# A two-layer graph attention kernel: the first part written as a hand-ordered pipeline of node tiles, with list work in pieces between them

## The chip, the cores and the metric

The kernel runs on one core of a Trainium2 chip. A core has a matrix engine (TensorE, PE in the profile; its weight loads are PEld), VectorE (DVE), ScalarE (ACT), GpSimd (POOL) and SyncE (SP), which here only issues DMAs. All engines run their own instructions in order and wait for each other through semaphores; DMAs move data between the device memory and the on-chip SBUF. The metric is the device time of one execution in microseconds (us). The time before is 2451.34 us, the median of 9 runs (2443.16 to 2461.27).

## The reference

There are 3125 nodes with 768 features each, and 53125 directed edges (each of 25000 pairs both ways, and a self loop per node), sorted by destination. What is computed, without the parameters' shapes:

```python
h  = relu(layernorm(x))                     # 3125 x 768
xl = h @ W1                                 # 3125 x 1024, 4 heads of 256
e  = leaky_relu((xl.a_src1)[src] + (xl.a_dst1)[dst], 0.2)
alpha = softmax of e over the edges with one dst
g  = segment_sum(xl[src] * alpha, dst) + b1
h1 = relu(layernorm(g) * g1 + be1) + (h @ Wr1 + br1)
# second layer: the same with W2 (1024 x 768) and one head
out = x + layernorm(gat(h1)) * g2 + be2 + (h1 @ Wr2 + br2)
```

## The kernel before, in words

The nodes are cut into 25 tiles of 125 (P = 125, NB = 25), and each tile gets a window of S = 2304 edge slots, 18 columns (J) of 128. The work of the first layer goes through these stages.

**First part (L586 to L669).** For each node tile, `transposed(b)` computes mean and variance on DVE (`norm_stats`: L316, L318), the square root on ScalarE (L322), the reciprocal and the scaling on DVE (L326, L600), transposes the tile on PE (L604) and takes the relu on ScalarE into `h0` (L606). Eight tiles `xt` are loaded ahead; the load of tile b + 8 is issued when tile b has been transposed. `alphas(b)` multiplies the transposed tile by the folded attention vectors `wa1` (L614, 12 matmul records) and copies 8 columns into `asad1` (L616). `products()` is a generator of 100 steps, four to a tile; one step is three chunks of `h @ W1` for one half of the tile's 1024 columns (L626, six matmul records). After each half ScalarE copies it into `row` (L629, two buffers), and a full row is stored to `table1` by SP (L146, L147); whole groups of `h0` go to `h0T_d` (L634).

Beside the tiles the first part holds three other pieces of work:
- `edge_list` (L197): loads `dst` and `src`, casts them, counts on DVE how many destinations lie below each tile (25 times L218, then L221 and L222), sums the counts with one matmul (L226), sets `starts` and the flag (L228 to L240), and splits the sources (L242 to L246).
- `fold` (L295): `wa1` from W1 and the attention vectors. For each of six chunks of W1 and each of two vectors GpSimd multiplies 128x1024 elements (L300), and ScalarE sums each of four heads (L304).
- `windows` (L248): SP reads each tile's start into a register (L177) and issues two list loads (L256, L257), 50 in all. DVE casts them (L260), PE transposes them (L263), DVE copies them back (L264) and computes the slots' indices (L266 to L271), and `keep` is stored four times (L277).

The order of PE's instructions is the written one (`manual_schedule(engines={PE})`, L641). The other engines' instructions are ordered by the framework's scheduler, which takes what is ready and prefers what was written earlier. Written order: the edge list's loads, four tiles with two product steps, the rest of the edge list, the fold, ten product steps, then tiles 4 to 24, each with the alphas of the tile four before and one product step; `windows` stands ahead of tile 12. So 33 product steps are written in the first part.

**Softmax (L332, called at L671).** A loop over 25 tiles loads two broadcast lists, compares them with node numbers on DVE (L374, L376, L379, L381), picks values with matmuls (L391, L399) and reduces on DVE (L393, L396, L401); then come scans over all slots (L452 to L479) with PE transposes between (L433, L444). Product steps are interleaved: one or two for a tile, then 8, 2, 8 and 2. What is left of them follows at L678.

**Between softmax and the sums.** W2 is folded on DVE in the pool "wf" (L681 to L691), which ends ahead of L693. Then comes the residual product of the first four tiles (L693 to L700): eight products of `wr1` and `h0[0]` into three PSUM buffers `pm` (L698). `copy_residual` copies each on ScalarE into the staging tile `rt` (L576), which belongs to the pool `mp` and has one buffer for two products, and every second copy is followed by four stores (L580). SP issues all of these loads and stores.

**Sums (L485, called at L782)**: GpSimd gathers the rows of `table1` for each column of slots (L524), ScalarE and DVE scale them (L542, L543), PE adds them up by one-hot matrices (L547, L559); the residual product of the other tiles runs between (L728). Its pools open after the first part's pools have closed. The second layer has the same stages.

A pool takes the place on top of those that are open, and a pool that opens after another has closed takes its place; unless it has `reuse_waits="tile"`, its first use waits for all work on the closed pool's tiles.

Of the kernel before, what the change touches and what calls it, by code (L numbers as in the profile page):

```python
# [58 lines left out]
def in_order(  # L59
# [137 lines left out]
    def edge_list(ep, pe):  # L197
# [18 lines left out]
        for b in range(NB):  # L216
            less = ep.tile([P, F], BF16, name="less", bufs=3)
            nc.vector.tensor_scalar(less, d16, float(b * P), 0.0, op0=OP.is_lt, op1=OP.add,  # L218
                                    accum_out=cnt[:, b:b + 1])
# [6 lines left out]
        nc.tensor.matmul(p_c[:1, :NB + 1], ones, cnt, start=True, stop=True)  # L226
        tot = ep.tile([1, NB + 1], F32, name="tot")
# [12 lines left out]
        nc.vector.tensor_copy(flag, flag_f)  # L240
        s_f = ep.tile([P, F], F32, name="s_f")
# [6 lines left out]
    def windows(pe):  # L248

        with tc.tile_pool(name="wn", bufs=1) as ep:  # L250
# [7 lines left out]
            for t, to in ((k16, dst_s), (s16, src_s)):  # L258
                tf = ep.tile([NB, S], F32, name="tf")
                nc.vector.tensor_copy(tf, t)  # L260
                pt = pe.tile([128, 512], F32, name="pe")
                for j in range(J):
                    nc.tensor.transpose(pt[:, j * NB:(j + 1) * NB], tf[:, j * 128:(j + 1) * 128], ident[:NB, :NB])  # L263
                nc.vector.tensor_copy(to.rearrange("p (b j) -> p j b", j=J),  # L264
# [4 lines left out]
            nc.vector.tensor_copy(idx_s, src_s)  # L269
            q, _ = divided(ep, src_s, [128, NB * J], "sh")  # L270
            nc.vector.tensor_copy(hi_s, q)  # L271

            keep = ep.tile([NB, S + 2], BF16, name="keep")
# [21 lines left out]
    def fold(abs_, w, nk, heads, cols, to):  # L295

        for k in range(nk):
            for m in range(2):
                t = abs_[2 + m % (len(abs_) - 2)]
                nc.gpsimd.tensor_tensor(t, w[:, k, :heads * cols], abs_[m], OP.mult)  # L300
                t = t.rearrange("p (h c) -> p h c", h=heads)
                for h in range(heads):
                    o = m * heads + h
                    nc.scalar.activation(t[:, h, :], t[:, h, :], AF.Copy, accum_out=to[:, k, o:o + 1])  # L304

    def norm_stats(pool, z, n):

        for _ in norm_steps(pool, z, n):
            pass
        return norm_steps.found  # L310
# [260 lines left out]
    with tc.tile_pool(name="m1", bufs=1) as mp:  # L571
# [10 lines left out]
        with tc.tile_pool(name="w1", bufs=1) as wp, tc.tile_pool(name="pm1", bufs=1, space=PSUM) as pm1:  # L582
# [3 lines left out]
            with tc.tile_pool(name="d1", bufs=2) as dp, tc.tile_pool(name="pd1", bufs=1, space=PSUM) as pp:  # L586
# [6 lines left out]
                def transposed(b):  # L593
# [5 lines left out]
                    mu, rstd = norm_stats(dp, xt, D)  # L599
                    nc.vector.tensor_scalar(xt, xt, mu, rstd, op0=OP.subtract, op1=OP.mult)  # L600
# [9 lines left out]
                def alphas(b):  # L610
# [5 lines left out]
                    nc.vector.tensor_copy(asad1[:, b, :], pa)  # L616
# [21 lines left out]
                AHEAD = 8  # L638
                EARLY = 4
                order = ctx.enter_context(ExitStack())  # L640
                order.enter_context(tc.manual_schedule(engines={PE}))  # L641
                with tc.tile_pool(name="el", bufs=1) as ep:
                    for b in range(2):
                        fetch(b)
                    listed = edge_list(ep, pp)
                    next(listed)
                    for k in range(NK1):
                        (nc.scalar, nc.gpsimd)[k % 2].dma_start(w1[:, k, :], W1[k * 128:(k + 1) * 128, :])
                    for b in range(2, AHEAD):
                        fetch(b)  # L650
                    abs1 = folded(mp, H, C1, a_src1, a_dst1, "wr1", 2)
                    for b in range(EARLY):
                        transposed(b)
                        if b == EARLY - 1:
                            for _ in range(2):
                                next(fill)
                    for _ in listed:
                        pass
                fold(abs1, w1, NK1, H, C1, wa1)
                for _ in range(10):  # L660
                    next(fill)
                for b in range(EARLY, NB):
                    if b == 12:
                        windows(pp)
                    transposed(b)
                    alphas(b - EARLY)
# [675 lines left out]
```

## Time and profile before

| what | us |
|---|---|
| median of 9 runs | 2451.34 |
| the profiled execution, its own time | 2454.62 |
| its span, first to last instruction | 2452.8 |
| mean granted PE clock, share of full | 0.955 |
| PE busy over the span | 2245.8 |
| DVE busy | 1921.4 |
| ACT busy | 1299.5 |
| POOL busy | 1174.4 |

The profile is of one execution. Its first table gives the busy time of each engine, and its second cuts the span into 40 slices of 61.3 us with the busy share of each engine in tenths (9 is 90% or more); PEclk is the clock that PE was granted. In lists of stretches each engine's busy time is followed by its number of instructions in brackets. In lists of waits the waiting instruction stands left of the arrow and what ended the wait right of it, with the sum, the number of times and the longest; "SPq" is SP's queue of DMA issues. An fp32 matmul shows as two records. The first part lies from 0 to 225 us, softmax from 225 to 490, the residual product of the first four tiles from 510 to 550.

### The profile page before, as it was taken

The numbers are of one execution on the slowest core, as the hardware profiler recorded it, in microseconds if no ns is written. First come the engines' busy times: TensorE is split into PE (matmuls) and PEld (weight loads), VectorE is DVE, ScalarE is ACT, GpSimd is POOL, SyncE is SP. The second block draws the span as 40 slices with busy tenths as digits, with TensorE's granted clock in tenths as the row PEclk, the third lists the DMA queues.
The fourth block names the chain that finished last, engine by engine and source line by source line (L and its number), as shares of the span: only waits on it lengthen the run. The fifth ranks groups of instructions, "written<-read, shape, count | busy, mean of one in ns | idle before, by whom it ended". The sixth has DMA issues, their size and how long they took to land.

```text
span 2452.8 us, 35967 instructions
## 1 busy us (share of the span) xinstructions
PE 2245.8 (92%) x11254; PEld 1481.3 (60%) x11254; DVE 1921.4 (78%) x4304; ACT 1299.5 (53%) x2783; POOL 1174.4 (48%) x995
## 2 busy tenths in 40 slices
PE   4858999998999999999999999799898999998987
PEld 2446655445666666666666776466565666666665
DVE  7433999847888888898989999587677687777777
ACT  3312332217888888888888898001244444444443
POOL 4200000015656555555655775000477777777775
PEclk9868999998999999999999999899999999998998
DMA  4235553269888888888988897784688988888886
GB/s 159 87 109 180 192 194 106 90 219 334 306 297 315 300 311 303 299 316 284 324 283 310 320 337 273 288 296 161 203 307 307 314 302 301 297 297 298 291 284 212
DMA packets 185506, 637.94 MB, mean 260 GB/s; under 512 B 31924, under 2 KB 49189, under 8 KB 184542
## 3 DMA queue, kind: packets, MB, share of 16 engines
q0 software_dynamic: 104464, 422.46, 49.9%
q1 hardware_dynamic: 76564, 201.94, 23.5%
q10 hardware_dynamic: 4282, 11.18, 1.3%
q8 instruction: 93, 1.52, 0.2%
q14 instruction: 103, 0.84, 0.1%
HBM read 567.40 MB, written 68.08 MB: 259 GB/s over the span
## 4 chain that ended last, share of the span: by engine, by line
PE 70%; DVE 16%; issue 5%; DMA 4%; ACT 2%; POOL 1%; SPq 1%; DVEq 0%; another core or an unknown queue 0%; ACTq 0%; POOLq 0%
PE pa L547 21%; PE p L773 11%; PE pa L559 8%; PE pr L728 8%; PE pr L807 7%; PE pm L626 6%; DVE g L543 3%; DVE scr L393 2%; DVE al L396 2%; PE pm L698 2%; PE pas L614 1%; DMA g<-table,idx_s 1%; PE pq L391 1%; PE pa L563 1%; DMA bs<-slo_d 1%
## 5 line engine op out<-in xcount | busy, mean ns | idle before, releaser
L524 POOL DMA_INDIRECT g<-table,idx_s x900 | 1072.1, 1191 | 892.5 <-ACT rt L576 338.5
L542 ACT ACTIVATE hi<-g,al 128x256 fp32r<-128x256 f32 (+1 forms) x1925 | 968.3, 579 | 511.0 <-DMA g<-table,idx_s 199.5
L543 DVE SCALAR_TENSOR_TENSOR g<-g,al,hi 128x256 fp32r<-128x256 f32 (+1 forms) x1925 | 993.2, 566 | 98.8 <-issue 64.2
L547 PE MATMUL pa<-hi,oh 128*125 128x512 f32 (+1 forms) x1450 | 586.3, 483 | 21.7 <-issue 12.6
L547 PE MATMUL pa<-g,oh 128*125 128x512 f32 (+1 forms) x1450 | 448.4, 386 | 27.3 <-issue 20.1
L547 PEld LDWEIGHTS pa<-hi,oh 128*125 128x125 f32 x1450 | 269.3, 190 | 206.0 <-issue 104.6
L547 PEld LDWEIGHTS pa<-g,oh 128*125 128x125 f32 x1450 | 269.4, 190 | 87.3 <-issue 29.3
L807 PE MATMUL pr<-wr,h 128*125 128x384 f32 x800 | 308.8, 517 | 7.3 <-issue 6.4
L559 PE MATMUL pa<-g,w 128*125 128x384 f32 (+1 forms) x900 | 289.3, 452 | 13.7 <-issue 8.1
L773 PE MATMUL p<-w,h1T 128*125 128x384 f32 (+1 forms) x800 | 298.5, 492 | 1.5 <-DVE h1T L764 1.5
L535 DVE TENSOR_SCALAR oh<-iota_f,rel_s 128x128 fp32r<-128x128 f32 x775 | 212.2, 284 | 109.0 <-PE pa L547 86.6
L626 PE MATMUL pm<-w,h 128*125 128x512 f32 x600 | 276.9, 612 | 15.4 <-ACT row L629 15.4
L728 PE MATMUL pr<-h0k,wr 128*128 128x500 f32 (+1 forms) x576 | 259.7, 536 | 7.6 <-DMA h0k<-h0T_d 7.6
L559 PEld LDWEIGHTS pa<-g,w 128*125 128x125 f32 x900 | 169.5, 192 | 96.6 <-issue 45.3
L807 PEld LDWEIGHTS pr<-wr,h 128*125 128x125 f32 x800 | 155.2, 199 | 95.9 <-issue 28.4
L626 PEld LDWEIGHTS pm<-w,h 128*125 128x125 f32 x600 | 111.2, 192 | 140.6 <-issue 123.7
L773 PEld LDWEIGHTS p<-w,h1T 128*125 128x125 f32 x800 | 148.0, 188 | 79.2 <-issue 10.9
L391 PEld LDWEIGHTS <-ohs 125*128 125x128 bf16 x2700 | 103.2, 99 | 59.1 <-DVE ohs L379 38.7
L728 PEld LDWEIGHTS pr<-h0k,wr 128*128 128x128 f32 x576 | 106.4, 191 | 52.5 <-DMA h0k<-h0T_d 11.1
L391 PE MATMUL pq<-tabs,ohs 125*128 125x100 bf16 (+1 forms) x2700 | 107.2, 194 | 33.0 <-DVE ohs L379 25.1
L511 DVE SCALAR_TENSOR_TENSOR z<-own,aw,pa 125x256 f32<-125x256 f32 (+1 forms) x150 | 69.8, 521 | 61.1 <-PE pa L547 31.7
L629 ACT ACTIVATE row<-pm 125x512 f32<-125x512 f32 x50 | 29.6, 596 | 161.9 <-PE pm L626 128.8
(192 smaller groups left out, 1679.3 us busy)
## 6 DMA issues: line engine op xcount, KB each, us to landing
bd<-dst_d SPq DMA_DIRECT2D x50, 576.0 KB
bs<-slo_d SPq DMA_DIRECT2D x50, 576.0 KB
g<-table,idx_s POOLq DMA_INDIRECT x900
r1T_d<-rt SPq DMA_DIRECT2D x100, 125.0 KB
r1t<-r1T_d SPq DMA_DIRECT2D x25, 500.0 KB
h1T_d<-h1T SPq DMA_DIRECT2D x25, 500.0 KB
h<-h1T_d SPq DMA_DIRECT2D x25, 500.0 KB
own<-table SPq DMA_DIRECT2D x24, 512.0 KB
```

Source lines behind the costliest of these rows:

```text
L391: nc.tensor.matmul(q[:, j], ohs[:P, (j0 + j) * 128:(j0 + j + 1) * 128], tabs[:, i], start=(i == 0), stop=(i == 2))
L511: nc.vector.scalar_tensor_tensor(z[:, o:o + n], own[:P, o:o + n], aw[:, o // cols:o // cols + 1], pa[:, o // f, o % f:o % f + n], op0=OP.m ...
L524: nc.gpsimd.indirect_dma_start(out=gf, out_offset=None, in_=table[:, :], in_offset=bass.IndirectOffsetOnAxis(ap=idx_s[:, c:c + 1], axis=0))
L535: nc.vector.tensor_scalar(oh, iota_f, rel_s[:, c:c + 1], None, op0=OP.is_equal)
L542: nc.scalar.activation(hi[:, cs], gf[:, cs], AF.Copy, scale=a)
L543: nc.vector.scalar_tensor_tensor(g[:, cs], gf[:, cs], a, hi[:, cs].bitcast(F32), op0=OP.mult, op1=OP.subtract)
L547: nc.tensor.matmul(pa[:, i, :f], oh[:, :P], t[:, i * f:(i + 1) * f], start=(j == 0 and t is hi), stop=False)
L559: nc.tensor.matmul(pa[:, o // f, o % f:o % f + n], w[:, o // cols, :], gf[:, o:o + n], start=(j == 0), stop=False)
L626: nc.tensor.matmul(pm[:P], h0[gi][:, k, o:o + P], w1[:, k, i * 512:(i + 1) * 512], start=(k == 0), stop=(k == NK1 - 1))
L728: nc.tensor.matmul(pm[:, :nb * P], wr1[:, k, m * 128:(m + 1) * 128], loaded[gi, k][:, :nb * P], start=(k == 0), stop=(k == NK1 - 1))
L773: nc.tensor.matmul(pm[:, :n], hT[:, k, :], w2[:, k, o:o + n], start=(k == 0), stop=(k == NK2 - 1))
L807: nc.tensor.matmul(pm[:, :384], h1[:, k, :], wr2[:, k, i * 384:(i + 1) * 384], start=(k == 0), stop=False)
```

## The change

The diff, cut to its core:

```diff
@@ edge_list and windows: points where the work is cut into pieces
         for b in range(NB):
+            if b % 9 == 0:
+                yield
             less = ep.tile([P, F], BF16, name="less", bufs=3)
...
         nc.tensor.matmul(p_c[:1, :NB + 1], ones, cnt, start=True, stop=True)
+        yield
...
         nc.vector.tensor_copy(flag, flag_f)
+        yield
...
             for t, to in ((k16, dst_s), (s16, src_s)):
-                tf = ep.tile([NB, S], F32, name="tf")
+                yield
+                tf = ep.tile([NB, S], F32, tag="tf", name="tf")
...
+                yield
                 nc.vector.tensor_copy(to.rearrange("p (b j) -> p j b", j=J),
...
-            keep = ep.tile([NB, S + 2], BF16, name="keep")
+            keep = ep.tile([NB, S + 2], BF16, tag="tf", name="keep")
@@ fold
             for m in range(2):
-                t = abs_[2 + m % (len(abs_) - 2)]
-                nc.gpsimd.tensor_tensor(t, w[:, k, :heads * cols], abs_[m], OP.mult)
-                t = t.rearrange("p (h c) -> p h c", h=heads)
-                for h in range(heads):
-                    o = m * heads + h
-                    nc.scalar.activation(t[:, h, :], t[:, h, :], AF.Copy, accum_out=to[:, k, o:o + 1])
+                t = abs_[2 + m]
+                nc.vector.tensor_tensor(t, w[:, k, :heads * cols], abs_[m], OP.mult)
+                nc.vector.tensor_reduce(to[:, k, m * heads:(m + 1) * heads],
+                                        t.rearrange("p (h c) -> p h c", h=heads), axis=AX.X, op=OP.add)
+            yield
@@ the first part (transposed(b) is split into stats, normal and flip)
+                AHEAD, LAG = 8, 10
+                def beside():
+                    with tc.tile_pool(name="el", bufs=1) as ep:
+                        listed = edge_list(ep, pp)
+                        next(listed)
+                        yield
+                        for _ in listed:
+                            yield
+                    lists = windows(pp)
+                    next(lists)
+                    yield from fold(abs1, w1, NK1, H, C1, wa1)
+                    for _ in lists:
+                        yield
+                work = beside()
...
+                with tc.manual_schedule(engines={ACT, DVE}):
+                    fetch(0)
+                    fetch(1)
+                    next(work)
+                    for b in range(2, 4):
                         fetch(b)
                     abs1 = folded(mp, H, C1, a_src1, a_dst1, "wr1", 2)
...
+                    late = None
+                    for b in range(-2, NB + LAG):
+                        if b + 2 < NB:
+                            stats(b + 2)
+                        if b == -1:
+                            for k in range(NK1):
+                                nc.scalar.dma_start(w1[:, k, :], W1[k * 128:(k + 1) * 128, :])
+                        if 0 <= b + 1 < NB:
+                            normal(b + 1)
+                        if 0 <= b < NB:
+                            flip(b)
+                        if b >= 0:
+                            next(work, None)
+                        if late is not None:
+                            late()
+                            late = None
+                        for _ in range(0 if b < 2 else 2 if b < LAG else 1 if b < NB or b % 2 else 0):
+                            next(fill)
+                        if b >= LAG:
+                            late = alphas(b - LAG)
+                    late()
+                    for _ in work:
                         pass
+                    for _ in range(3):
+                        next(fill)
@@ the residual product of the first four tiles
+                rp = order.enter_context(tc.tile_pool(name="rf", bufs=1))
                 for m in range(NK2):
                     if m % 2 == 0:
-                        rt = mp.tile([128, GB, 2, P], F32, name="rt", bufs=1)
+                        rt = rp.tile([128, GB, 2, P], F32, name="rt0", bufs=4)
...
-            order.close()
+                order.close()
```

In words: in the first part the instructions of ScalarE and DVE now keep the written order too. A turn b of the loop holds the statistics of tile b + 2, the scaling of tile b + 1, the transposes of tile b, one piece of the other work, the copy of the alphas of the turn before, product steps and the alphas of tile b - 10. The pieces are: the casts of the lists (turn 0), the counting in three pieces (1 to 3), the flag (4), the split of the sources, the 50 list loads and the first chunk of the fold (5), the other chunks (6 to 10), the casts and transposes of the slot lists and their indices (11 to 16). The fold runs on DVE, a multiply and a reduction for each vector and chunk. All six chunks of W1 are loaded from ScalarE's queue, after the second square root; before, three were issued by ScalarE and three by GpSimd at the start. There are 39 product steps in the first part: 2 a turn from turn 2 to 9, 1 a turn from 10 to 24, 1 every other turn to 34, and 3 at the end. The staging tiles of the first residual product lie in a pool of their own, "rf", with four buffers, and it closes together with PE's manual order.

## The prediction

> **What bounds the kernel now.** I first read the 40 slices of the page. TensorE (PE) is at 9 tenths nearly everywhere; the only low digits ahead of slice 28 are in slices 0 to 3, which is the part that the change rewrites.
>
> ```profile
> span 2452.8 us, 35967 instructions
> PE   4858999998999999999999999799898999998987
> DVE  7433999847888888898989999587677687777777
> PEclk9868999998999999999999999899999999998998
> ```
>
> Then I read the busy time of each engine in stretches that I cut where PE stops and starts (start:end, length, then PE, PEld, DVE, ACT and POOL busy, granted clock, DMA share, GB/s).
>
> ```profile
> 57.00:72.40 15.40, 0.02 (x1) 0.02 (x1) 6.18 (x5) 11.78 (x56) 13.11 (x6) 0.59 0.01 2
> 72.40:85.00 12.60, 12.60 (x24) 5.42 (x25) 8.43 (x25) 3.13 (x10) 0.00 (x0) 0.82 0.28 84
> 121.50:146.70 25.20, 0.00 (x0) 0.00 (x0) 3.21 (x7) 0.88 (x2) 0.00 (x0) 0.56 0.14 48
> 146.70:162.10 15.40, 13.04 (x60) 9.69 (x61) 8.90 (x15) 0.97 (x2) 0.54 (x1) 0.50 0.53 206
> 162.10:216.60 54.50, 54.50 (x290) 36.57 (x289) 13.59 (x41) 14.72 (x35) 2.70 (x5) 1.00 0.42 151
> 225.50:412.10 186.60, 166.82 (x2004) 112.72 (x2004) 185.38 (x270) 65.48 (x67) 0.00 (x0) 0.96 0.50 171
> 510.00:550.50 40.50, 40.44 (x97) 18.05 (x95) 21.33 (x32) 5.38 (x9) 11.46 (x11) 1.00 0.66 220
> ```
>
> Two holes stand out, 15.4 and 25.2 us without PE work, and each is followed by a stretch at a low clock. From 162 to 217 PE is the bound, from 225.5 to 412 (the softmax loop) VectorE (DVE) is, with 185.38 of 186.60 us. The list of waits names what ends the holes.
>
> ```profile
> PE pm L626 <- ACT row L629: 15.4, 1, 15.4
> PE pe L263 <- DVE tf L260: 27.6, 2, 25.3
> DVE tf L260 <- DMA k<-dst_d: 21.5, 1, 21.5
> SPq L146 <- ACT row L629: 81.4, 7, 17.9
> ```
>
> The first: the copy of `row` on ScalarE stands behind the fold, which goes back and forth between GpSimd (L300) and ScalarE (L304) and ends at 71.7. The second: PE stands at the transposes of the slot lists, which wait for the list loads, the last of them issued at 143.8. Those loads came late because SyncE (SP), in order, waited with `row` stores among them (17.9 us at the longest).
>
> **The first part, step by step.** PE's work there is known from its chain: 0.65 us for a tile's transposes, 1.21 for its alphas, 2.67 for a product step, together 4.53 (the cycle from 162 to 217). Before, softmax begins on DVE at 225.5. When does it after?
>
> *Start.* DVE is now held to the written order, so stats(2), normal(1) and the casts of the lists come one after the other. Before, the lists landed at 18.9 and 21.2, behind weights that are now issued only after the second square root (9.4). I take 17 for the end of these casts; the ends are 14 and 22. An issue can be held up by another queue's transfer (that of `s_i` waited 2.6 us on a load of W1), so ScalarE may stand at the six weight loads for some us. All 8 MB must come anyway, and from 4 to 22 us the DMA share is about 1, so I let products start near 24 (31 before).
>
> *Fold on DVE.* Removed: 12 GpSimd multiplies at 2.36 us and 48 ScalarE sums at 0.40 + 0.19. Added on DVE: 12 multiplies and 12 reductions of 128x1024. The same pair on 128x768 (L690, L691) takes 0.95 and 0.94 busy, 0.87 from start to start; scaled by 1024/768 that is 1.13 each, 4.5 a chunk, 27 in all.
>
> *DVE up to the fold's end.* A tile's statistics and normalization cost 2.1 (bn_stats 1.02, bn_aggr 0.20, reciprocal 0.16, scaling 0.68). Counting pieces are 9 at 0.515 = 4.64. So turns 1 to 3 take 6.7 + 6.7 + 6.8, turn 4 (flag) 4, turn 5 (2.1 + 4.9 for the slot split + 4.5) 11.5, turns 6 to 10 6.6 each: 69 us. PE needs only 0.65 + 2 x 2.57 = 5.8 in those turns, so DVE sets the pace and the first alphas, which need the whole fold, come at 17 + 69 = 86. PE idles about 9 us ahead of them.
>
> *SP, the queue that is passed.* The 50 list loads are now written at turn 5, ahead of the stores of rows 1 to 3. They can begin some 3.3 us after the store of `l16` as before (51.7 to 55.1), about 53; before, unhindered pairs took 0.8 us (register already loaded) or 1.65, so 25 pairs take 20 to 41 us and end at 73 to 94. I take 84. DVE asks for them at about 91, so the 21.5 us wait goes. In return row 1's store stands behind them, `row` has 2 buffers, so ScalarE, now in order, stands at row 3's copy from about 71 to 87, and with it the square root that DVE needs in turn 10. That delays the fold's end by about 4 (0 to 16). First alphas: 90.
>
> *The rest.* Turns 11 to 24: 14 cycles of 4.53, two times 2.1 for the list transposes, 1.7 for the first wait on `tf`, 1.2 for alphas(0): 71 us, so 161. Then ten alphas at 1.63 (the spacing when they stood alone at 216 to 220) and five product steps at 2.67: 29, so 190. The softmax masks that were computed early (L381, 2 x 0.61) now come after: +1. Softmax begins at 191 instead of 225.5: **34 us less**; with the ends above, 18 to 42. The three product steps at the end (7.7 us) lie beside DVE's softmax prologue (225.5 to 231.4, 7.1 us with the masks); at most 0.6 shows. Through the softmax loop the steps per tile are the same and DVE stays the bound: no change.
>
> **Between softmax and the sums.** 39 product steps are done ahead of softmax instead of 33 (of 100), so after softmax's last transposes (471.5) 9 are left instead of 15, and PE comes to the residual product (L698) 6 x 2.57 = 15.4 us sooner, at 494.8 on the old clock. Its weights are in by 484, where the DMA traffic of their load ends. This looks like a gain; I expect it is lost, because of where the four staging tiles lie. `rt` lived in `mp`, a place of its own. The pool "rf" opens after "wf" (the W2 fold on DVE) has closed and takes its place. That such a successor waits is seen twice:
>
> ```profile
> SPq L684 <- DMA alo_d<-own: 2.6, 1, 2.6
> POOL g L524 <- DVE w2t L690: 10.2, 1, 10.2
> L691 DVE TENSOR_REDUCE wa2s<-w2t x16: 942/944/947, 503.6 to 528.7; 128x1 f32<-128x768 f32 x16
> ```
>
> The loads of "wf" waited for softmax's store, and the gathers into the sums' buffers wait for `w2t`. The W2 fold ends at 529.6, and that hangs on softmax's end, not on PE. So three products fill the three PSUM buffers by 510, PE stands until 529.7, ScalarE copies (0.68), and five products of 5.04 remain: 530.4 + 25.2 = 555.6, against 550.4 before. PE has then been idle about 20 us. After the hole of 15.4 us the 24 matmul records took 12.84 us where the chain's pace of 0.429 gives 10.3, so 2.6 more: 558.2. **8 us more**; 5 if the clock recovers at once, 12 if the sums' first buffers, which now lie over "rf", also wait for its last store (such a store held the next copy up to 8.1 us before). Behind it SP's chain (bias, W2, h0k) follows L698's end by 22.4 us as before.
>
> Here a page speaks against the change. The Trainium skill, "TensorE: Matmul & The Clock Gate", section on the HAM clock gate, says that an idle window of about 3.4 us puts PE at half clock until a busy window has passed. The rows agree in direction (0.82 and 0.50 after the holes). By the rule one restart costs at most about 1.7 us, an estimate from that page, and the second term would be 7 in place of 8.
>
> Four staging tiles themselves save nothing on PE: it shows 40.44 of 40.50 us with one. ScalarE's waits for stores (20.3 us) lay beside it.
>
> From 600 to 1400 PE is busy 799.7 of 800 us, and nothing there is changed, so the difference is carried to the end.
>
> **Sum.** -34 + 8 = -26. The profiled execution took 2454.62 (span 2452.8 and 1.8 around it), which gives 2428.6; it lies 3.3 above the median of 2451.34, so in terms of the median **2425**.
>
> **Rivals.**
>
> 1. *No wait at "rf".* If its tiles lie elsewhere or wait only for tiles long dead, the six steps are a gain, cut by about 2 where the sums' buffers wait for the last store: -34 - 13 = -47, so 2404. For it: the loads of `wr1` are done by 484. Against it: the two waits above. Chance 0.18.
>
> 2. *In order hurts more.* Lists landing as late as before (22) cost 5; ScalarE standing the full 16 costs 12 more than I took; -34 + 17 + 8 = -9, so 2442. For it: SP waited 81.4 us on `row` in this part. Chance 0.14.
>
> 3. *Slower, by the list loads.* DVE is now in order through turn 11. If the loads come as late as before (last landing 145.3), not only the lists but also the normalization behind them stands, which before was done ahead. From there 14 turns with the transposes, 68, the tail 29 and the masks 1: softmax at 243.3, +18 + 8 = +26, so 2480. It decides from a landing at about 117, 26 us later than DVE asks. For it: SP is in order and row stores did hold these loads. Against it: they are now written ahead of those rows. Chance 0.11.
>
> That the change does not do what it says, the holes merely passing from GpSimd to DVE, is in rival 2 and in the 9 us that I count.
>
> **Numbers.** Forecast 0.57, rivals 0.18, 0.14, 0.11. The range goes down past rival 1 with a somewhat better start, 2398, and up to rival 2 with the dearer restart, 2448; it leaves out rival 3 and little else. Measurement tells 0.3% (7 us) from no change: faster means below 2444. Forecast, rival 1 and a little of rival 2 give 0.78, the rest of rival 2 gives 0.10 for no change, rival 3 with a margin 0.12 for slower.
>
> **What would show it.** Right: no hole at 57 or 121; the first alphas near 90 and softmax's first cast near 190; the fold's pair at 1.2 us busy each; PE standing some 20 us at L698 behind L691, and the first `rt0` copy just after the W2 fold. Wrong: a long wait at `tf` for `k`, ScalarE standing at `row` for over 20 us, or L698 running without a hole.

## The result and the profile after

The changed kernel takes 2464.5 us (median of 14 runs) where the kernel before, run beside it, takes 2451.9 (46 runs): ratio 1.0053, 95% interval 1.0043 to 1.0063, so it is **slower** by 13 us, half a per cent. The forecast was 2425.

The page's slices after; the lines that answer to those of before:

```profile
span 2462.5 us, 35867 instructions
...
PE   3898999958999999999999999799989989989997
...
DVE  5845999647889898888888999587677787777787
...
PEclk9998999988999999999999999899989999999999
```

Slices 0 to 3 are fuller together (28 tenths for 25), as they should be, and both holes are gone. But slice 8, counted from 0 (493 to 554 us), has fallen from 8 to 5: a new hole, behind the softmax. The same in stretches (start:end, length, PE, PEld, DVE, ACT and POOL busy, granted clock, DMA share, GB/s), cut where the changed kernel's stages turn:

```profile
85.00:105.00 20.00, 12.14 (x34) 5.82 (x32) 16.87 (x23) 2.94 (x8) 1.07 (x2) 0.74 0.52 170
105.00:173.80 68.80, 67.11 (x386) 45.98 (x384) 37.88 (x97) 19.17 (x47) 4.34 (x7) 1.00 0.47 171
173.80:220.00 46.20, 44.81 (x173) 26.86 (x173) 9.72 (x29) 11.25 (x12) 0.00 (x0) 0.78 0.36 120
498.20:520.90 22.70, 0.09 (x1) 0.00 (x0) 22.11 (x27) 0.69 (x2) 0.00 (x0) 0.62 0.28 87
520.90:548.00 27.10, 26.98 (x60) 11.96 (x60) 0.00 (x0) 3.88 (x7) 0.00 (x0) 0.94 0.17 57
```

PE is the bound from 105 on. In the tail (third line) it is busy 44.81 of 46.20 us, and yet its clock is 0.78. The fourth line is the new hole: 22.7 us without PE, while DVE does the W2 fold. The list of waits, first part and then 480 to 700 us:

```profile
ACT bn_sd L604 <- DMA w<-in_L_gnn_W_dram: 18.3, 1, 18.3
...
ACT row L648 <- DMA table<-row: 14.2, 1, 14.2
```

```profile
POOL g L525 <- DVE oh L536: 62.8, 1, 62.8
ACT rt L577 <- DVE wa2s L731: 36.4, 1, 36.4
DVE oh L536 <- DMA r1T_d<-rt: 31.7, 1, 31.7
...
PE pm L739 <- ACT rt L577: 22.7, 1, 22.7
```

The second fence is one chain, read from below: PE's residual product waits for the first staging copy, the copy for the W2 fold; behind it the sums' first one-hot tile waits for the staging's last stores, and by this list the gathers stand behind that tile (run 13 below shows that this last link is not the whole of it). Marks of both traces, in us from the span's start (the forecast's shift where it gave one):

| mark | before | changed | shift | forecast |
|---|---|---|---|---|
| softmax's first cast on DVE | 225.5 | 211.0 | -14.5 | -34 |
| its first picks on PE | 229.9 | 219.9 | -10.0 | -34 |
| W2 fold's end | 529.6 | 520.1 | -9.5 | -34 |
| residual product, end | 550.4 | 547.9 | -2.5 | -26 |
| second gather and those behind it | from 529 | from 553 | +24 | |
| sums' tile 0, 1, 2, bias product | 596.9, 636.8, 677.3 | 599.7, 642.0, 691.4 | +2.7, +5.1, +14.2 | -26 |
| sums' tile 24 | 1535.1 | 1549.2 | +14.1 | -26 |
| end of the span | 2452.8 | 2462.5 | +9.7 | -26 |

The gathers' first lines behind the W2 fold, before and changed:

```profile
528.64 0.96 POOL L524 DMA_INDIRECT g<-table,idx_s  x1 [10.24 <-DVE w2t L690]
```

```profile
553.24 0.97 POOL L525 DMA_INDIRECT g<-table,idx_s  x1 [62.79 <-DVE oh L536]
```

So the first part gave 10 us where 34 were forecast, and from the W2 fold's end to tile 2 the kernel lost 24 where 8 were.

### The profile page after: what moved, and what is told of

Its sections match the earlier page's. It is cut to its first block, busy times and chain, and to the rows that moved or that the text cites. A ratio compares the mean times of both kernels' runs of the same rounds, so it can differ in the third digit from the quotient of the medians.

```text
span 2462.5 us, 35867 instructions
## 1 busy us (share of the span) xinstructions
PE 2247.7 (91%) x11254; PEld 1473.8 (60%) x11254; DVE 1942.1 (79%) x4328; ACT 1277.1 (52%) x2687; POOL 1142.4 (46%) x980
## 4 chain that ended last, share of the span: by engine, by line
PE 67%; DVE 17%; issue 6%; DMA 6%; ACT 2%; SPq 1%; POOL 1%; DVEq 0%; ACTq 0%; POOLq 0%; another core or an unknown queue 0%
PE pa L548 21%; PE p L814 10%; PE pa L560 8%; PE pr L769 8%; PE pr L848 7%; PE pm L645 5%; DVE g L544 2%; DVE scr L394 2%; DMA g<-table,idx_s 2%; DVE al L397 2%; PE pq L392 2%; ACT hi L543 1%; PE pas L633 1%; PE pa L564 1%; PE pm L739 1%
## 5 line engine op out<-in xcount | busy, mean ns | idle before, releaser
L848 PE MATMUL pr<-wr,h 128*125 128x384 f32 x800 | 302.2, 508 | 10.9 <-issue 8.4
L645 PE MATMUL pm<-w,h 128*125 128x512 f32 x600 | 284.9, 625 | 0.0
L392 PE MATMUL pq<-tabs,ohs 125*128 125x100 bf16 (+1 forms) x2700 | 105.9, 193 | 26.7 <-DVE ohs L380 22.7
```

The source lines that it names most:

```text
L392: nc.tensor.matmul(q[:, j], ohs[:P, (j0 + j) * 128:(j0 + j + 1) * 128], tabs[:, i], start=(i == 0), stop=(i == 2))
L645: nc.tensor.matmul(pm[:P], h0[gi][:, k, o:o + P], w1[:, k, i * 512:(i + 1) * 512], start=(k == 0), stop=(k == NK1 - 1))
L848: nc.tensor.matmul(pm[:, :384], h1[:, k, :], wr2[:, k, i * 384:(i + 1) * 384], start=(k == 0), stop=False)
```

## Experiments

The kernel before took 2452 us beside the changed one, 2460 to 2461 beside runs 1 to 8 (on chip 0) and 2409 to 2412 beside the rest (chips 12 and 14). So I compare ratios to it, and marks of the trace up to the sums' tile 2; in run 14, the changed kernel again, these come within 3 us of the first trace, so smaller differences of these marks tell nothing by themselves. In the table, ratio with its 95% interval, then the first cast, the first picks and tile 2, in us.

| run | ratio | cast | picks | tile 2 |
|---|---|---|---|---|
| changed kernel | 1.0053 (1.0043 to 1.0063) | 211.0 | 219.9 | 691.4 |
| 1 e1_old_staging | 0.9913 (0.9898 to 0.9928) | 209.0 | 218.1 | 655.7 |
| 2 e2_own_place | 0.9965 (0.9950 to 0.9979) | 212.4 | 221.3 | 672.4 |
| 3 e3_before_rf | 1.0100 (1.0084 to 1.0115) | 225.1 | 229.5 | 701.4 |
| 4 e4_w1_pool | 1.0029 (1.0016 to 1.0042) | 203.0 | 212.1 | 681.4 |
| 5 f1_bias_late | 0.9890 (0.9873 to 0.9906) | 204.8 | 213.8 | 653.8 |
| 6 f2_tail | 0.9933 (0.9913 to 0.9953) | 203.8 | 225.7 | 668.0 |
| 7 f3_rows_pool | 0.9915 (0.9900 to 0.9930) | 208.0 | 217.1 | 654.6 |
| 8 e8_old_all | 0.9895 (0.9873 to 0.9917) | 207.4 | 216.6 | 654.5 |
| 9 g1_windows_late | 0.9909 (0.9890 to 0.9928) | 203.8 | 211.3 | 651.2 |
| 10 g2b_alphas_spread | 0.9929 (0.9909 to 0.9949) | 201.2 | 218.1 | 659.4 |
| 11 g2a_all | 0.9933 (0.9911 to 0.9956) | 197.9 | 215.7 | 655.8 |
| 12 h1_old_fold | 0.9969 (0.9955 to 0.9982) | 216.0 | 225.1 | 664.8 |
| 13 k1_rf_one | 1.0052 (1.0035 to 1.0069) | 213.0 | 221.8 | 693.3 |
| 14 k0_after_again | 1.0045 (1.0026 to 1.0063) | 213.7 | 222.8 | 691.6 |
| 15 k2_tail_cut | one execution, 2369.7 us | 192.9 | 200.4 | 638.6 |

The first cast has a trap. The tail is the stretch from the first product step behind the last node tile to that cast. In the changed kernel and in runs 1, 2, 4, 5, 7, 8, 9, 12, 13 and 14 PE has the same work in it, and yet it takes 33.6 to 33.7 us in runs 1, 4 and 7 and 37.0 to 37.3 in the others, at different granted clocks. The changed kernel's and run 1's:

```profile
173.80:211.00 37.20, 35.81 (x153) 23.15 (x153) 7.03 (x18) 8.44 (x9) 0.00 (x0) 0.76 0.42 139
```

```profile
175.30:209.00 33.70, 32.31 (x153) 21.55 (x153) 7.01 (x18) 8.44 (x9) 0.00 (x0) 0.84 0.46 151
```

What decides between the two lengths no run shows, and none of these edits touches the tail. So the start of the tail is the better mark for what an edit did ahead of it: 173.8 in the changed kernel (176.7 in run 14), 175.3 in run 1, 169.4 in run 4, 167.6 in run 5, 174.3 in run 7, 170.4 in run 8, 166.9 in run 9, 179.0 in run 12.

**The staging: runs 1, 2, 3, 13, 14.** Run 1 undoes it:

```
-                rp = order.enter_context(tc.tile_pool(name="rf", bufs=1))
-                        rt = rp.tile([128, GB, 2, P], F32, name="rt0", bufs=4)
+                        rt = mp.tile([128, GB, 2, P], F32, name="rt", bufs=1)
```

> The changed kernel with the residual staging as it was: one buffer in m1, no pool rf. All else of the change stays. Theory A (the new pool takes wf's place, so the first residual waits for the end of the W2 fold, and the sums start behind it): the residual's products start when the first layer's products end (483 us instead of 521) and, at the 40.4 us that they took in the kernel before, end near 524; the sums' tile 2 comes between 650 and 663 instead of 691.4; time 2423 to 2436, some 28 to 41 us below the changed kernel. Theory B (the sums' start is bound by something else of the new order, the gathers or the list, and the wait at rf only stands beside it): the sums' tile 2 stays at 685 to 692, time 2458 to 2466.

Theory A. The ratio falls by 0.014 (34 us) and the kernel is faster than before. Stretches and GpSimd's timeline of run 1 (start, length, idle time before in brackets):

```profile
500.00:520.00 20.00, 20.00 (x48) 8.76 (x47) 19.11 (x30) 2.72 (x4) 2.97 (x3) 1.00 0.47 149
520.00:540.00 20.00, 13.70 (x34) 8.27 (x33) 12.67 (x36) 17.61 (x44) 12.88 (x15) 0.74 0.99 351
540.00:560.00 20.00, 6.47 (x13) 3.20 (x14) 5.35 (x15) 0.82 (x3) 0.87 (x1) 0.66 1.03 406
```

```profile
516.42 0.96 POOL L525 DMA_INDIRECT g<-table,idx_s  x1 [29.11 <-ACT rt L577]
```

PE and the W2 fold on DVE run side by side (20.00 and 19.11 of 20 us), and the gathers go out from 516 on. Not all of PE's lead is kept: from 540 to 560 PE waits 13.6 us for a `h0k` load while the DMA share is 1.03.

Run 2 opens "rf" ahead of "wf":

```
+                rp = order.enter_context(tc.tile_pool(name="rf", bufs=1))
                 with tc.tile_pool(name="wf", bufs=2) as fp:
...
-                rp = order.enter_context(tc.tile_pool(name="rf", bufs=1))
```

> The changed kernel with the pool rf opened ahead of the pool wf, so that it has a place of its own: four buffers, no wait for the W2 fold. Theory A: the residual's products run from 483 to 510 or so at their 27 us, nothing stands at the copies; tile 2 at 645 to 663, time 2418 to 2436, as the old staging or up to 5 us better. Theory B: as the changed kernel, 2458 to 2466. A third case: the sums wait for the W2 fold's end (520) in any event, because their pools lie where wf lay; then this kernel and the one with the old staging end alike, within 3 us.

Neither: it gains about half of what run 1 does at tile 2 (19.0 of 35.7 us). The residual product no longer waits, but with four buffers it takes 484.7 to 525.1, the same 40.4 us as with one. So four buffers save nothing on PE, as said ahead. What remains is that the sums' tiles now lie over "rf":

```profile
DVE oh L536 <- DMA r1T_d<-rt: 17.4, 2, 16.8
```

but the gathers go out from 520.1, right behind the W2 fold, so tile 0 (579.7) is only 3.6 us behind run 1's. Tile 2 is 16.7 behind; 9.3 of that arise between tile 1 and tile 2, of which more below. Run 3 is the kernel before with the new staging alone (the edit of run 1 the other way round, on the kernel before).

> The kernel before with nothing but the new staging (pool rf behind wf, four buffers, closed inside the with). Theory A: the residual's first copy waits for the W2 fold's end (529.6), the products end near 557 instead of 550.4, and the sums' tile 2 comes 8 (my prediction's price) to 24 us (what the changed kernel's trace shows from the W2 fold's end to tile 2) later; time 2459 to 2476. Theory B: no cost of its own, 2449 to 2454; the loss belongs to the first part's new order.

Theory A: 1.0100, tile 2 24.2 us later, on the unchanged first part. The residual's end comes at 556.9 (+6.5), where I had priced 8; the other 18 lie behind it. On the changed first part the staging costs more, 35.7 us at tile 2 from run 1 to the changed kernel, and 27.8 of them already at the residual's end: there the wait for the W2 fold also takes PE's lead. The waits of run 3, 500 to 700 us:

```profile
DVE oh L535 <- DMA r1T_d<-rt: 31.8, 1, 31.8
...
ACT rt L576 <- DVE wa2s L691: 18.9, 1, 18.9
```

Runs 13 and 14 were made to split these two prices: run 13 is the changed kernel with `bufs=4` made `bufs=1` in "rf", run 14 the changed kernel again.

> The changed kernel with the pool rf where it is, behind wf, but one staging buffer instead of four (4 KB a partition instead of 16). Theory A (two prices: the place costs the wait for the W2 fold, and the 16 KB cost a second one, since the sums' first one-hot tiles lie over them and wait for the last stores; the gathers then start at 553 instead of 529): the first residual copy still comes right behind the W2 fold's end at about 520 and the residual ends at 548 to 553, but VectorE no longer stands at the first one-hot tile for r1T, the gathers start by 532, and tile 2 comes at 670 to 684 instead of 691.4; ratio to the kernel before 0.997 to 1.003. Theory B (the wait for the W2 fold alone costs all, what lies behind it only follows): tile 2 at 689 to 697, ratio 1.003 to 1.008. Theory C (the four buffers were needed: with one the copies wait for stores and the residual takes its 40 us behind the fold): residual's end at 560 or later, ratio above 1.008.

> The changed kernel again, unaltered, beside the one with one staging buffer. If the chip makes no difference to the ratio: 1.003 to 1.008 to the kernel before, and every mark up to the 25th tile of the first sums within 3 us of the first profile (first part cast 211, W2 fold's end 520, tile 2 691).

Theory B by the numbers: runs 13 and 14 are alike. But not by B's reason alone. With one buffer (4 KB) the first one-hot tiles are free at 522.7, as theory A had it, and yet the gathers come no sooner. DVE's line in run 13, and its waits, 480 to 700 us:

```profile
522.72 1.65 DVE L536 TENSOR_SCALAR oh<-iota_f,rel_s 128x128 fp32r<-128x128 f32 x8
```

```profile
POOL g L525 <- DMA g_c<-in_L_gnn_g_dram: 64.4, 1, 64.4
...
DVE oh L536 <- ACT w L558: 29.3, 1, 29.3
```

The second gather goes out at 557.1, behind SyncE's issue of the last staging stores at 552.5 to 554.3 (the load of `g_c`, to which the list puts the wait down, is issued right behind them). So freeing the one-hot tiles is not enough; the gathers lie behind the residual's last stores in any kernel that has "rf" in wf's place (553, 557, 556 and 562 in the changed kernel, runs 13, 14 and 3), and early where the staging stays in m1 (529 before, 516 in run 1). Which tile ties them in run 13 the trace does not name. The rest is the order that goes with "rf": in the six kernels that have it (the changed one, runs 2, 3, 4, 13 and 14) tile 2 follows tile 1 by 49.5 to 50.7 us, in all others by 40.4 to 40.5. It is not the time at which the sums start: run 2 reaches tile 1 at 622.7 and has the 49.7, run 6 reaches it at 627.5 and has 40.5. In the changed kernel, 600 to 665 us:

```profile
DVE iso L507 <- issue: 9.9, 1, 9.9
```

DVE stands at 641 to 651, in order, at the `iso` of a later tile, whose values GpSimd gathers only at 644; tile 1's `z` stands behind it. In the six kernels this stand takes 9.0 to 10.9 us; runs 1 and 6 and the kernel before have at most 1.6 there. That "rf" brings about this order is argued, as no run changed the order alone. More than one buffer in m1 itself was not tried.

**The start: runs 4, 5, 8.** Run 4 issues the W1 loads from GpSimd (`nc.scalar.dma_start(w1...` becomes `nc.gpsimd.dma_start(w1...`).

> The changed kernel with the six W1 loads issued by GpSimd instead of ScalarE. Theory A (ScalarE stood from 6.5 to 25.0 us at issuing them, and the first tiles' square roots behind it): the first bn_sd comes at about 12, the first layer's first product some 8 us earlier than 33.1, the first part's end 3 to 10 us earlier, time 2454 to 2461. Theory B (the biases' halving that stands on VectorE at 23.8 to 30.5 us, and the list's chain, set the first part): the first product moves by less than 2 us, the time by less than 2: 2462 to 2466.

Theory A by the time only: the ratio falls by 0.0024 (6 us). The first product comes 3.7 us earlier (29.4), where 8 were expected, and of the 8.0 at the first cast 3.6 are the shorter tail, so 4.4 come from the start. ScalarE's wait of 18.3 us for the loads has made room for one of 17.8 for VectorE: GpSimd issues the W1 loads from 1.6 to 9.8, and `x`'s third tile lands 3.5 us later than in the changed kernel, whose line stands first:

```profile
19.61 1.02 DVE L600 BATCH_NORM_STATS2 bn_st<-xt 125x6 f32<-125x384 f32 x2 [11.86 <-DMA xt<-in_x_dram]
```

```profile
23.14 1.02 DVE L600 BATCH_NORM_STATS2 bn_st<-xt 125x6 f32<-125x384 f32 x2 [15.55 <-DMA xt<-in_x_dram]
```

Run 5 takes run 1 and moves `split_biases(mp)` from behind the softmax to the end of the manual part. In the changed kernel's timeline of DVE (and in run 1's) it had been put into the middle of turn 1:

```profile
30.47 0.17 DVE L165 CAST b_hi<-b_v 128x8 fp32r<-128x8 f32 x1 [6.69 <-DMA b_v<-in_L_gnn_b_dram]
```

> The kernel with the old staging (the whole first part as changed), and the biases' halving (its loads, casts and differences) written at the end of the first part instead of behind the softmax. Theory A (VectorE, written out in order, stood 6.7 us at the biases' load ahead of the second tile's scaling, and everything of the first part lies behind it): the second tile's scaling comes some 6 us earlier, the part casts begin at 201 to 205 instead of 209.0, the span falls by 4 to 8 us from 2429.8. Theory B (what follows is set by the list and by SP's list loads, 69 to 95 us, which do not move): casts within 1.5 us of 209, span within 2 us.

Theory A for the first part: first product 5.5 earlier, the tail's start 7.7, the first cast 4.2, since run 5 has the long tail and run 1 the short one. The span of its profile is 4 longer than run 1's, lost behind tile 24, where nothing differs; the ratios, 0.9890 and 0.9913, overlap. Run 8 has both repairs on run 1.

> The old staging, the W1 loads from GpSimd and the biases late, all three. If the three terms add (8 us of the start for the W1 loads, 4 to 8 for the biases): casts at 194 to 200, span 2414 to 2422, ratio to the kernel before 0.985 to 0.989. If the two repairs of the start cover each other (VectorE and ScalarE stand in the same 6.5 to 30 us): casts at 200 to 203, span 2419 to 2426.

Worse than either forecast at the cast (207.4). The tail begins at 170.4, no earlier than with the biases alone (167.6). The two repairs do not merely cover each other: the third tile of `x` lands at 22.6 here and at 19.0 in run 5, with the W1 loads again issued by GpSimd from the start. That these push it back is argued from the times.

**The tail and the clock: runs 6, 10, 11, 15.** Run 6 puts the tail's ten alphas in a block and the eight product steps behind them:

```
-  ... 2 if b < LAG else 1 if b < NB or b % 2 else 0):
+  ... 2 if b < LAG else 1 if b < NB else 0):
...
-                    for _ in range(3):
+                    for _ in range(8):
```

> The kernel with the old staging, and in the tail behind the last node tile the ten alphas in one block, then the eight steps of products together. Theory A (the 128x8 matmuls, though PE is shown busy, let the granted clock fall, and products set between them pay double: 4.4 to 5.5 us a step instead of 2.6 to 2.8): the products, in one block, run at half clock only in their first step or two, 8 steps in 22 to 27 us instead of 23.4 + 9.4; the casts begin at 193 to 198, the first pq some 2 to 8 us earlier than 218, the span falls by 2 to 8. Theory B (the clock is lost to something else in these 40 us): all eight steps at 4.4, 35 us, the first pq at 222 to 232, the span 4 to 12 us longer.

A's mechanism with B's price. Stretch and timeline of run 6:

```profile
180.00:200.00 20.00, 18.36 (x83) 17.70 (x83) 3.32 (x10) 2.22 (x2) 0.00 (x0) 0.50 0.17 60
```

```profile
176.60 2.69 PE L633 MATMUL pas<-wa,h 128*125 128x8 f32 x12 [0.26 <-DVE asad L635]
...
202.78 19.63 PE L645 MATMUL pm<-w,h 128*125 128x512 f32 x40
```

(The second line is cut off by the end of its window at 222 us.) With nothing but 128x8 matmuls PE is busy 18.36 of 20 us and the clock is 0.50; an alphas group takes 2.69 us instead of 1.37. The products behind run at full pace after the first, 22.9 us for eight steps, as forecast; but the alphas cost 30 us instead of 16, and the picks come 7.6 later. Run 10 (run 5 with two alphas a turn from turn 11 on, none left for the tail):

> Old staging, biases late, and the alphas that are left over at turn 10 made up between turns 11 and 20, two a turn with a product step between, so that none is left behind the last tile and the tail holds products alone. Theory A (the clock falls where 128x8 matmuls stand for most of the time, as in the block of ten at 2.69 us each; mixed one by one with products and transposes they run at 1.4 to 1.5 and cost no clock): the granted clock stays at 0.95 or more from 100 to 200 us, the casts begin at 188 to 195 instead of 204.8, the first pq at 200 to 208 instead of 213.8, span 2420 to 2428. Theory B (PE's work is the bound and 128x8 matmuls cost the same wherever they stand): the casts earlier by what the eight product steps behind them take, but the first pq within 2 us of 213.8, and the span within 3 us of 2434.

Theory A fell. Mixed with products the 128x8 matmuls still cost the clock: 0.66, 0.90, 0.84, 0.83 in the 20 us stretches from 100 to 180 (run 5: 1.00, 1.00, 1.00, 0.91), and the picks come 4.4 later than in run 5. In the last two of these stretches PE has no idle time to blame:

```profile
140.00:160.00 20.00, 20.00 (x105) 13.68 (x104) 9.32 (x24) 4.43 (x11) 1.09 (x2) 0.84 0.26 87
160.00:180.00 20.00, 20.00 (x103) 13.56 (x102) 6.35 (x20) 3.95 (x10) 0.00 (x0) 0.83 0.21 87
```

One alphas group a turn, as in the changed kernel's turns 11 to 24, keeps the clock at 1.00. Run 15 cuts the last ten alphas to one chunk of six:

```
+                    n = NK1 if b < 15 else 1
-                    for k in range(NK1):
+                    for k in range(n):
```

> The kernel with the old staging; the alphas of the last ten tiles take one of their six chunks only (they leave out five sixths of the sum). Theory A (the 128x8 matmuls bring the granted clock down, and the product steps between them pay): the five product steps among them take 2.6 to 3.0 us each instead of 2.8 to 5.5, the granted clock from 180 on stays at 0.95 or more, and the tail from the last tile's product step to the first part cast takes 15 to 20 us instead of 37. Theory B (the steps are slow there for another reason): the steps stay at 4.3 to 4.5, and the tail shortens only by what the left-out matmuls took, about 13 us, to 24 or so.

Theory A, clearly. Tail of the changed kernel, then of run 15, and run 15's stretch:

```profile
176.42 1.37 PE L633 MATMUL pas<-wa,h 128*125 128x8 f32 x12
...
179.39 4.51 PE L645 MATMUL pm<-w,h 128*125 128x512 f32 x6
...
187.15 5.46 PE L645 MATMUL pm<-w,h 128*125 128x512 f32 x6
```

```profile
177.97 0.28 PE L634 MATMUL pas<-wa,h 128*125 128x8 f32 x2
178.51 0.38 PE L634 MATMUL pas<-wa,h 128*125 128x8 f32 x2 [0.26 <-DVE asad L636]
178.75 2.82 PE L646 MATMUL pm<-w,h 128*125 128x512 f32 x6
```

```profile
180.00:200.00 20.00, 18.88 (x56) 9.24 (x55) 7.88 (x25) 10.43 (x11) 0.00 (x0) 1.00 0.61 214
```

The steps take 2.82 instead of 4.51 to 5.46 and the clock stays at 1.00 up to 200 us. The tail is 18 us instead of 37 (34 in run 1). The left-out matmuls are 11 us at full clock (ten times five sixths of 1.37); the rest, 8 us, or 5 against run 1, goes with the clock.

**What bounds turns 4 to 12: runs 7, 9, 11, 12.** Run 7 stores the first four rows from GpSimd (`store_rows(nc.gpsimd if b < 4 else nc.sync, table1, b, row)`).

> The kernel with the old staging, and the first four rows' stores issued by GpSimd instead of SyncE. Theory A (row 1's store lay on SP behind the 50 list loads, 69 to 95 us, ScalarE stood 14 us at row 3's copy, and VectorE's fold and the first alphas stood behind ScalarE's next square root): the stand goes, first alphas at 94 to 99 instead of 104, casts 3 to 8 us earlier, span 3 to 8 us shorter. Theory B (the fold's own 27 us and the windows' transposes set the first alphas, as tf's data come at 107 in any case): first alphas within 2 us of 104, span within 2 us.

The stand is gone and the first alphas begin at 95, but that mark misleads: they stop at the last chunk of the fold. PE's timeline in run 7:

```profile
95.11 1.26 PE L633 MATMUL pas<-wa,h 128*125 128x8 f32 x10
102.67 0.59 PE L633 MATMUL pas<-wa,h 128*125 128x8 f32 x2 [6.30 <-DVE wa L309]
...
107.95 5.03 PE L645 MATMUL pm<-w,h 128*125 128x512 f32 x6
```

The fold ends 2.3 us sooner (102.6 for 104.9), the tail and the casts begin 1.0 sooner, and the time is the same: theory B in the time. ScalarE's stand of 14 us cost about 2 at the fold's end and nothing that can be told behind it. Run 9 is run 5 with the rows on GpSimd, and with three empty pieces between the fold and the slot lists.

> Old staging, biases late, the first four rows' stores on GpSimd, and the slot lists' first piece (tf) three turns later on VectorE. Theory A (with the store's stand gone, what holds turn 11 is VectorE standing in order at tf for the list loads that SP ends at 95 to 107: the run with the rows on GpSimd alone had its first alphas at 95 but the next ones at 113): the second alphas come within 8 us of the first, the casts at 194 to 200 instead of 204.8 with the biases late alone, the span 4 to 10 us below 2434.0, ratio 0.984 to 0.988. Theory B (PE, 19 to 20 us busy of each 20 from 100 on, is the bound whatever the order): casts within 2 us of 204, ratio 0.988 to 0.991.

Theory B: casts at 203.8. The fold ends at 97.2 and the alphas' last chunk waits for it; DVE is busy 19.51 of 20 us from 80 to 100. In turns 6 to 10 the bound is DVE with the fold, afterwards PE. Run 11 has runs 9 and 10 together.

> All four: old staging, biases late, rows' stores on GpSimd and slot lists three turns later, alphas spread. If the gains add: first pq at 192 to 200, span 2410 to 2420, ratio 0.979 to 0.985. If the spread alphas take the room that the later lists freed: first pq at 200 to 206, ratio 0.984 to 0.989, as the better of the two parts.

Neither: picks at 215.7, the spread alphas cost more than the rest gives. Run 12 puts the fold back on GpSimd and ScalarE, in run 1.

> The old staging, and the W1 fold again as GpSimd's multiplications and ScalarE's accumulating copies, in the pipelined order. Theory A (in turns 4 to 10 PE, busy 20.0 of 20 us from 60 to 80, sets the pace and not VectorE, so the fold's engine does not matter): first alphas within 4 us of 104.1, casts within 3 us of 209.0, span within 4 of 2429.8. Theory B (VectorE with its 29 us of fold sets it): first alphas 6 to 15 us earlier, casts 4 to 12 earlier. Theory C (48 copies of 0.4 + 0.19 us on ScalarE and 12 products of 2.4 on GpSimd, in the queues that hold the tiles' square roots, copies and the x loads, hold the tiles up): first alphas 5 to 25 us later, casts 4 to 20 us later, ratio 0.993 to 1.0.

Theory C by the cast, 7.0 later, and by the ratio, higher by 0.0056 (13 us). Of the 7.0, 3.3 are the longer tail and 3.7 arise ahead of it; the first alphas come only 2.5 later (106.6), which is theory A's mark. So the ratio shows that the fold on DVE is a gain, but not by which path.

The best version is run 5, the changed first part with the old staging and the biases late: 0.9890 (0.9873 to 0.9906), faster than both kernels, though not told apart from runs 1, 7, 8 and 9.

## Why the prediction was wrong, point by point

**Start.** Step "I take 17 for the end of these casts" failed: 22.6, just past my end of 22, since `x`'s third tile landed at 19.6. I had said that ScalarE may stand at the weight loads; it did, for 18.3 us. What that cost is not settled: with the loads on GpSimd the tail begins 4.4 us earlier in run 4, but no earlier in run 8 than in run 5, and `x`'s third tile lands later in both. Not in my list at all was the next turn: 13.7 us instead of 6.7, since the biases' casts, written behind the softmax, were put into DVE's queue there and waited 6.7 us. Run 5, without them, begins its tail 7.7 us earlier than run 1.

**Fold.** 27 us said (0.87 scaled by 1024/768 is 1.16 and not 1.13, so the sum should have read 27.8); each of the 24 measures 1.22 busy and a pair 2.4 from start to start, 28.7 in all. Near enough, and run 12's time shows that DVE was the better place. From turn 1's end to the fold's end: 66.3 said with the 4 for ScalarE, 68.7 measured.

**SP.** Right: no wait at `tf` for the list, row 1's store behind the list loads, ScalarE standing 14.2 us at row 3's copy. Its price of 4 measures 2.8 as DVE's wait for the square root ahead of the last chunk, and 2.3 and 1.7 at the fold's end in runs 7 and 9.

**The rest.** Turns 11 to 24: 71 said, 68.8 measured. The tail failed: "ten alphas at 1.63 ... and five product steps at 2.67: 29", with the mask 30, against 37.2 (the terms add up to 29.7). I took both durations at full clock; beside so many 128x8 matmuls the clock was 0.76 and a step 2.8 to 5.5 (runs 6, 10, 15). In the runs with the short tail the miss would have been 3.5 us less. The row that I took the 1.63 from had the sign in it. The kernel before ends its first part with four alphas in a block, and only the first two of them keep that pace:

```profile
216.59 1.37 PE L614 MATMUL pas<-wa,h 128*125 128x8 f32 x12
218.22 1.47 PE L614 MATMUL pas<-wa,h 128*125 128x8 f32 x12 [0.26 <-DVE asad L616]
219.95 2.35 PE L614 MATMUL pas<-wa,h 128*125 128x8 f32 x12 [0.26 <-DVE asad L616]
222.65 2.66 PE L614 MATMUL pas<-wa,h 128*125 128x8 f32 x12 [0.35 <-DVE asad L616]
```

The last three steps, "at most 0.6 shows", also ran slow (9.4 us), and the picks came 8.9 us behind the first cast instead of 4.4. Together: 5.6 + 7.0 + 2.4 - 2.2 + 7.2 = 20.0 for the cast, and 4.5 behind it: -34 became -10.

**Staging.** The place, the wait and PE's hole were right: copies at 520.2 right behind the fold at 520.1, the residual's end 27.8 us behind it (28.6 said). The restart was priced too high: behind the hole 27.1 us ran at a clock of 0.94, by which about 1.6 us were lost (an estimate from that row), where I had added 2.6; the 1.7 that I had set beside it was nearer. The step that failed is the one after it: "Behind it SP's chain follows L698's end by 22.4 us as before", and the difference "is carried to the end". SP's chain did follow. GpSimd's gathers did not: before, ten of them were out by 541, under the residual product, and now the second goes out at 553. I had named this ("if the sums' first buffers, which now lie over "rf", also wait for its last store"), but priced it at 4. From the residual's end (-2.5) to tile 2 (+14.2) the kernel lost 16.7: 7.6 up to tile 1, behind the late gathers, and 9.1 between tile 1 and tile 2, at the stand for `iso`, which I had not in my list and whose cause is argued only. The term of 8 is 24.

**Sum.** -10 + 24 = +14 at tile 2, where I had -34 + 8. Of my rivals, the first, no wait at "rf", is run 1 in effect: -47 said, -21.6 at tile 2, since the first part gave less, and PE's lead ran into the `h0k` loads. The third, slower by late list loads, had the right sign by luck: the lists came in time.

The Trainium skill, "TensorE: Matmul & The Clock Gate", section "A second HAM failure mode: psum-queue depth-cycling", tells of another kernel, in which PE idles for very short times between groups of matmuls, often enough for the clock to swing between half and full. Run 6 (0.26 us idle in every 2.95, clock 0.50) would fit it. Run 15 has such a hole of 0.26 us in every 3.4 us, oftener than the changed kernel's tail (one in some 7.3), and its clock is 1.00 where the tail's is 0.76. So the holes alone do not do it here; run 15 differs by the narrow matmuls that it leaves out. The weight loads that go with them do not explain it either: they fill 45.98 of 68.80 us in turns 11 to 24, at clock 1.00, and 23.15 of 37.20 in the tail. That the width of 8 columns is what counts is what remains, and is not shown by itself.

## What to carry to other kernels

Before you give a transfer more staging buffers, look whether the engine that is the bound waits for the one it has; here PE was busy 40.4 of 40.5 us, so the new pool had nothing to give it, and it lost twice, at the work whose place it took and at the work that took its place. When a stage behind a change starts early, under other work, a later end of that work is not carried over one to one: ask what had been running ahead and what its buffers now lie over. When an engine is put in a written order, look for instructions from other parts that land in its queue, and take a matmul's time from a row with the same mix of widths around it.

## What the runs showed of the hardware

- Matmuls of 128x8, issued back to back with PE shown busy 18.36 of 20 us, brought the granted clock to 0.50 (run 6). One group of 12 matmul records in a turn of some 4.5 us left it at 1.00 (the changed kernel, 105 to 174 us, PE busy 67.11 of 68.80), two groups a turn at 0.83 and 0.84 with PE busy 20.00 of 20 us (run 10).
- The same PE work, ten such groups with five product steps between, took 33.7 us at a clock of 0.84 in one run and 37.2 at 0.76 in another (run 1 and the changed kernel).
- One queue stood 18.3 us at issuing six loads of 512 KB (ScalarE, with a DMA share of 0.96), and the square root behind them with it. Issued from GpSimd, and earlier, they stood less, but another load, `x`'s third tile, landed 3.5 us later (run 4).
- The same kernel took 2% less beside the later runs, which were on other chips (2452 to 2461 and 2409 to 2412 us for the one before). In the changed kernel nearly all of it lies behind the first layer's sums: its marks agree within 3 us up to tile 24 (1549.2 and 1547.2), then the spans are 2462.5 and 2422.5. What made the difference there was not followed.
